# Routing layer 0's experts from each tile's best 32 tokens, with gate rows spread by DMA and the full comparison kept as a branch

## The chip, the cores and the metric

The kernel runs on one core of one Trainium2 chip. The metric is the device time of one execution in microseconds (us); the kernel before has a median of 1907.97 us over 3 runs. Engines are called PE (TensorE), DVE (VectorE), ACT (ScalarE), POOL (GpSimd) and SP (SyncE, which mostly issues DMAs). Most data is float32.

## The reference, cut to what matters

A sequence of 2048 tokens of 256 numbers passes through four layers. Each has a cross-attention over a context of 1601 rows and a feed-forward part, both added to x. What changes is the feed-forward part of layer 0, a set of 8 experts:

```python
t = log(clip(layernorm(x) @ gate_w, 1e-6))          # 2048 x 8
for _ in range(8):                                   # Sinkhorn
    t = t - logsumexp(t, over tokens); t = t - logsumexp(t, over experts)
gates = exp(t)
vals, idx = top_k(gates.T, 256)                      # each expert takes its best 256 tokens
out[e] = (layernorm(x)[idx[e]] @ experts[e]) * vals[e]
routed = zeros_like(x).at[idx].set(out)              # a token taken twice keeps one of its results
x = x + routed
```

The masks of layer 1 and layer 3 (2048 x 1601, the same for every token here) hide only some of the last 400 context rows.

## The kernel before

Tokens are held as 16 tiles of 128 partitions, four tiles to a chunk of 512. x stays on the chip from start to end. `network` calls the stages in order: `attention0`, then `experts0`, `attention1_tail`, `ffn1`, `attention1` of layer 2, `ffn2` with `attention3_keys`, `attention3_tail` and `ffn3`. While `attention0` runs, a helper looks at the masks (`look_at_masks`). `verdict` (L301) sums what it found into an integer, all engines read it, and a branch (`tc.If(n_odd == 0)`) stands between `attention0` and everything else: in the ordinary case attention 1 and 3 use only the last 400 context rows for the masked part, in the other branch all stages treat the masks in full. `experts0` is the first stage inside either branch.

`experts0` (L522 to L782) has its order on each engine written by hand (`manual_schedule`), with one generator, `ahead`, that holds the dense work: for each of the 16 tiles, four product steps of four matmuls (L589), which together give all 8 experts' outputs of the tile's 128 tokens. ACT copies each step out of PSUM (L599), and after every second step SP writes half a tile's table, 512 KB, to DRAM (L602). `step(ahead, 1)` places one product step at that point of the order; there are 64. The stages around it:

- The norm of four chunks (`norm_steps`: statistics L151, L152, `rstd` on POOL L157, `xn` L171, transposes L185) and gate logits (L626), with 6 product steps.
- Eight Sinkhorn iterations on the gates `g`, 128 x 16 x 8 (L639 to L652), with a step each.
- The ranking (L658 to L745): a token's rank for an expert is the number of tokens with a larger gate. For each expert the 2048 gates are spread to all partitions (16 PE transposes L670, 4 ACT copies L674 into `bc`). Then each tile's gates are compared with the row, as per-partition scalars. For nine tiles a comparison and a sum are one DVE instruction (L710); for seven tiles DVE compares (L715) and ACT sums (L689). Each pair of tiles is compared once: sums along the row give one side, and counting matmuls with `pick` (L682), four concurrent column groups, give the other. 50 product steps stand between.
- `rank` (L742 to L745), the winners (L751 to L767): who is under 256, and for each token the expert whose result counts, as an `index` into its tile's table and a `gate`.
- Sixteen indirect fetches on POOL (L772) and DVE's `add_row` (L782), x += row * gate.

The layer 1 stage `attention1_tail` begins with constants of the masks on DVE (L963 to L970), projections of 400 context rows (keys L983 and casts L988, values L992 and copies L996), then chunk by chunk norm and query matmuls (L1006). Weight scratch comes from pools whose buffers are freed in turn; in layer 3, `bv`, `bo`, `spread`, `wvT` belong to pools of attention 3, and the first loads of `ffn3` (L1965) follow when such room is free.

Of the kernel before, what the change touches and what calls it, by code (L numbers as in the profile page):

```python
# [54 lines left out]
class Net:  # L55
# [245 lines left out]
    def verdict(self):  # L301

        nc = self.nc
        n = self.const.tile([1, 1], mybir.dt.int32, name="n_odd")
        with ExitStack() as s:
            self.banks(s)
            ps = self.pm()
            nc.tensor.matmul(ps[0:1, 0:1], lhsT=self.some, rhs=self.ones[:, 0:1], start=True, stop=True)
            nc.vector.tensor_copy(n, ps[0:1, 0:1])
        return nc.values_load(n[0:1, 0:1], min_val=0, max_val=P)  # L310

# [210 lines left out]
    def experts0(self):  # L522
# [3 lines left out]
        for kc in range(2):  # L526
            (w,) = self.weights(f"e0{kc}", 2048)
            ew.append(w.rearrange("p (e f) -> p e f", e=E))
            nc.sync.dma_start(
                ew[kc], a["L0_ffn_experts"][:, kc * P : (kc + 1) * P, :].rearrange("e p f -> p e f")  # L530
            )

        short = 7
        with ExitStack() as s:
            self.banks(s)
            pool = s.enter_context(tc.tile_pool(name="e0", bufs=1))
            bcp = s.enter_context(tc.tile_pool(name="e0b", bufs=2))
            cp = s.enter_context(tc.tile_pool(name="e0c", bufs=9))  # L540
            stage = s.enter_context(tc.tile_pool(name="e0s", bufs=3))
            rows = s.enter_context(tc.tile_pool(name="e0r", bufs=6))
            dram = s.enter_context(tc.tile_pool(name="e0d", bufs=1, space=bass.MemoryType.DRAM))
            gw = pool.tile([P, 2, E], F32, name="gw")
            nc.sync.dma_start(gw, a["L0_ffn_gate_w"].rearrange("(k p) e -> p k e", p=P))

            after = pool.tile([P, (NT - short) * P], BF16, name="after")
            nc.gpsimd.memset(after, 1.0)
            nc.gpsimd.affine_select(
                out=after[:, :P], in_=after[:, :P], compare_op=ALU.is_gt, fill=0.0, base=0,  # L550
                pattern=[[1, P]], channel_multiplier=-1,
            )

            rest = pool.tile([P, NT], F32, name="rest")
            nc.vector.tensor_reduce(rest[:, 0:1], after[:, :P], AX.X, ALU.add)
            for t in range(NT - 1, -1, -1):
                nc.vector.tensor_scalar(rest[:, t : t + 1], rest[:, 0:1], float((NT - 1 - t) * P), None, ALU.add)

            first = pool.tile([P, 1], F32, name="first")
            nc.vector.tensor_scalar(first, rest[:, NT - 1 :], float(-E), float(E * (P - 1) - 1), ALU.mult, ALU.add)  # L560

            pick = pool.tile([P, E, E], BF16, name="pick")
            nc.vector.memset(pick, 0.0)
            for e in range(E):
                nc.vector.memset(pick[:, e, e : e + 1], 1.0)

            fold = pool.tile([P, E], F32, name="fold")
            nc.vector.tensor_reduce(
                fold, self.ident.rearrange("p (k r) -> p r k", k=4)[:, :E, :], AX.X, ALU.add
            )  # L570
            none = pool.tile([P, CH], BF16, name="none")
            nc.gpsimd.memset(none, 0.0)
            number = pool.tile([P, E], F32, name="number")
            for e in range(E):
                nc.vector.memset(number[:, e : e + 1], e + 1.0)
            xnT = [pool.tile([P, 2, CH], F32, name=f"xe{c}") for c in range(NCH)]
            table = [dram.tile([P * E, D], F32, name=f"table{t}") for t in range(NT)]
            g = pool.tile([P, NT, E], F32, name="g")

            near = pool.tile([P, NT, E], F32, name="near")  # L580
            far = pool.tile([P, short, E], F32, name="far")
            seen = pool.tile([P, NTOK], BF16, name="seen")
# [10 lines left out]

            def ahead():
                todo = None

                def out():
                    t, h, y, ps = todo
                    nc.scalar.copy(y[:, h * 512 : (h + 1) * 512], ps)  # L599
                    if h % 2:  # L600
                        at = slice((h - 1) * 512, (h + 1) * 512)
                        nc.sync.dma_start(table[t].rearrange("(p e) d -> p (e d)", e=E)[:, at], y[:, at])  # L602

# [35 lines left out]
            for _ in range(8):  # L639
# [12 lines left out]
                nc.vector.tensor_tensor(g, g, ri.unsqueeze(2).to_broadcast([P, NT, E]), ALU.mult)  # L652

# [44 lines left out]
            for e in range(E):  # L698
# [6 lines left out]
                for n, t in enumerate(turns):  # L705
# [21 lines left out]
                    if n in (1, 3, 7, 9, 11, 15) or n == 13 and e < 2:  # L727
                        step(ahead, 1)
# [3 lines left out]
            drain(ahead)  # L732
# [8 lines left out]
            for t in range(NT):  # L741
# [5 lines left out]

            taken = pool.tile([P, NT, E], F32, name="taken")
            order = pool.tile([P, NT, E], F32, name="order")
            top = self.small.tile([P, NT], F32, name="top")  # L750
            nc.vector.tensor_scalar(taken, rank, float(M), None, ALU.is_lt)  # L751
            nc.vector.scalar_tensor_tensor(
                order, rank, float(E), number.unsqueeze(1).to_broadcast([P, NT, E]), ALU.mult, ALU.add
            )
            nc.vector.tensor_tensor(order, order, taken, ALU.mult)
            nc.vector.tensor_reduce(top, order, AX.X, ALU.max)
            nc.vector.tensor_tensor(order, order, top.unsqueeze(2).to_broadcast([P, NT, E]), ALU.is_equal)
            nc.vector.tensor_tensor(order, order, taken, ALU.mult)
            nc.vector.tensor_tensor(g, g, order, ALU.mult)

            nc.vector.tensor_tensor(taken, order, number.unsqueeze(1).to_broadcast([P, NT, E]), ALU.mult)
            nc.vector.tensor_reduce(top, taken, AX.X, ALU.max)
            nc.vector.tensor_scalar(top, top, 1.0, first, ALU.max, ALU.add)
            index = pool.tile([P, NT], mybir.dt.uint32, name="index")
            nc.vector.tensor_copy(index, top)
            gate = pool.tile([P, NT], F32, name="gate")
            nc.vector.tensor_reduce(gate, g, AX.X, ALU.add)  # L767

            fetched = []
            for t in range(NT):  # L770
                row = rows.tile([P, D], F32, name="row")
                nc.gpsimd.indirect_dma_start(  # L772
                    row[:], None, table[t][:, :], bass.IndirectOffsetOnAxis(ap=index[:, t : t + 1], axis=0)
                )
                fetched.append(row)
                if t >= 2:
                    self.add_row(t - 2, fetched[t - 2], gate)
# [7 lines left out]
    def attention1(self, pre, mask=None, bias=False, beside=None):  # L785

        tc, nc, a = self.tc, self.nc, self.a
        raw = {}
        for n, w in zip(("Wk", "Wv", "Wq"), self.weights(pre, 512, 512, 512)):
            raw[n] = w.rearrange("p (o i) -> p o i", o=2)  # L790
            self.load_rows(f"{pre}_{n}", D, raw[n])
        with ExitStack() as s:
# [6 lines left out]
            for n in ("Wk", "Wv", "Wq"):  # L799
                wT[n] = kv.tile([P, 2, D], F32, name=f"{n}T")  # L800
# [146 lines left out]
    def attention1_tail(self, pre, mask, beside=None):  # L947

        tc, nc, a = self.tc, self.nc, self.a
        raw = {}  # L950
# [1123 lines left out]
```

## Time and profile before

| | us |
|---|---|
| median of 3 runs (lowest, highest) | 1907.97 (1907.56, 1908.0) |
| the profiled execution's own time | 1902.67 |
| its span, first to last instruction | 1900.9 |
| PE, DVE, ACT, POOL busy | 1744.6, 994.3, 819.8, 689.8 |
| mean granted clock of PE | 0.963 |
| gates before Sinkhorn ready | 746.4 |
| Sinkhorn | 746.6 to 765.6 |
| ranking, first row transpose to last counts | 766.6 to 905.25 |
| index of winners ready | 914.6 |
| last `add_row` ends | 937.5 |
| first query matmul of layer 1 | 943.98 |

All times within a profile are of the one profiled execution and run from its span's start. In a group's line come line, engine, operation, output and inputs, shapes and count, then busy time and mean duration, then the idle time of the engine ahead of these instructions with what ended it. In a line of windows the columns are the stretch, its length, the busy time of PE, PE's weight loads, DVE, ACT and POOL, the granted clock of PE as a share of full speed, the DMA engines' busy share, and GB/s.

### The profile page before, as it was taken

The page shows a single profiled execution, that of the slowest core. Times are in us where ns is not written, and L with a number is a line of the kernel's source. Part 1 is how long each engine was busy: PE and PEld are TensorE (multiplying, and loading weights), DVE is VectorE, ACT ScalarE, POOL GpSimd, SP SyncE. Part 2 cuts the span into 40 slices and gives each one's busy share as a digit, 9 for nine tenths or more (in the row PEclk, how much of TensorE's full clock was granted, in tenths as well). Part 3 has the DMA queues.
Part 4 walks back from the last instruction along what each step waited for, and adds up shares of the span by engine and source line. Part 5 has one row for each costly group of instructions (what it writes and reads, how often), then busy time and mean ns, then how long its engine had stood idle before and what let it go on. Part 6 is the DMA issues. An engine that isn't in the chain of part 4 may idle for free.

```text
span 1900.9 us, 22408 instructions
## 1 busy us (share of the span) xinstructions
PE 1744.6 (92%) x8397; PEld 868.1 (46%) x8397; DVE 994.3 (52%) x2022; ACT 819.8 (43%) x1097; POOL 689.8 (36%) x473
## 2 busy tenths in 40 slices
PE   6779999999999978999699989999999879999798
PEld 3223333333333335443345864645666722333587
DVE  5555654664465424899574653332115477886200
ACT  4554444443443432799123541121125546666222
POOL 2057876976786861000400561011015600211100
PEclk9889999999999998999699999999999989999799
DMA  8840000000000011222310000000000000000651
GB/s 274 271 143 1 1 1 1 1 1 1 1 1 1 1 58 65 89 100 100 118 39 0 1 26 0 1 0 1 0 6 1 6 16 19 20 21 13 198 184 44
DMA packets 51171, 86.70 MB, mean 46 GB/s; under 512 B 9949, under 2 KB 36974, under 8 KB 51054
## 3 DMA queue, kind: packets, MB, share of 16 engines
q1 hardware_dynamic: 48480, 81.45, 13.1%
q0 software_dynamic: 768, 2.10, 0.4%
q10 hardware_dynamic: 1806, 1.64, 0.3%
q8 instruction: 68, 1.11, 0.3%
q14 instruction: 49, 0.40, 0.1%
HBM read 61.96 MB, written 18.87 MB: 43 GB/s over the span
## 4 chain that ended last, share of the span: by engine, by line
PE 39%; DVE 4%; ACT 3%; issue 2%; POOL 2%; DMA 1%; SPq 1%; ACTq 0%; DVEq 0%; POOLq 0%
PE psc L913 5%; PE pa L933 5%; PE psc L1826 4%; PE psc L1978 3%; PE pa L1989 3%; ACT p L1833 2%; PE pa L1297 2%; PE pa L1050 2%; PE psc L1040 2%; PE pa L1843 2%; PE psc L1378 1%; PE pm L880 1%; PE pm L185 1%; PE psc L922 1%; PE psc L1244 1%
## 5 line engine op out<-in xcount | busy, mean ns | idle before, releaser
L492 POOL TENSOR_TENSOR sp<-sp,p 128x1024 f32<-128x1024 f32 (+1 forms) x176 | 418.4, 2377 | 56.2 <-ACT p L476 45.5
L396 DVE TENSOR_REDUCE mp<-pm 128x1 f32<-128x512 f32 x384 | 242.7, 679 | 175.1 <-PE pm L391 174.3
L476 ACT ACTIVATE p<-psc 128x1024 f32<-128x1024 f32 (+1 forms) x208 | 212.7, 1023 | 264.6 <-PE psc L471 176.0
L471 PE MATMUL psc<-qT,kT 64*128 64x512 f32 (+1 forms) x832 | 219.9, 592 | 0.0
L483 PE MATMUL pa<-p,v 128*64 128x512 f32 (+1 forms) x832 | 202.8, 609 | 0.0
L1833 ACT ACTIVATE p<-psc 100x1024 f32<-100x1024 f32 x128 | 124.3, 1020 | 61.3 <-PE psc L1826 54.0
L1811 DVE TENSOR_REDUCE ms<-psc 128x2 bf16<-128x800 f32 x128 | 124.1, 987 | 42.8 <-PE psc L1807 41.2
L589 PE MATMUL pa<-w_e,xe 128*128 128x512 f32 x256 | 124.8, 615 | 4.9 <-ACT y L599 4.9
L391 PE MATMUL pm<-kb,qb 64*128 64x512 bf16 x384 | 99.3, 392 | 25.9 <-DVE mp L396 22.2
L483 PEld LDWEIGHTS pa<-p,v 128*64 128x64 f32 (+1 forms) x832 | 50.9, 137 | 131.9 <-issue 128.9
L913 PE MATMUL psc<-q,kT 128*128 128x512 f32 (+1 forms) x208 | 102.2, 610 | 0.0
L933 PE MATMUL pa<-v,p 128*128 128x257 f32 (+1 forms) x416 | 95.3, 382 | 0.0
L471 PEld LDWEIGHTS psc<-qT,kT 64*128 64x128 f32 (+1 forms) x832 | 85.0, 185 | 20.1 <-issue 6.6
L1826 PE MATMUL psc<-q,kT 32*100 32x512 f32 x512 | 81.0, 645 | 13.4 <-ACT p L1833 11.7
L156 POOL TENSOR_SCALAR rstd<-mv 128x4 f32<-128x4 f32 x32 | 9.4, 297 | 227.9 <-DVE mv L152 215.8
L171 DVE TENSOR_SCALAR xn<-x,mv,rstd 128x256 f32<-128x256 f32 x128 | 59.0, 517 | 62.2 <-PE pm L185 47.9
L469 PE MATMUL psc<-sh,negz 64*128 64x512 bf16 (+1 forms) x416 | 86.7, 384 | 5.1 <-ACT sh L418 4.2
L885 DVE TENSOR_REDUCE mp<-pm 128x1 f32<-128x512 f32 x64 | 34.3, 570 | 102.5 <-PE pm L880 102.3
L689 ACT ACTIVATE seen<-ge 128x1152 bf16<-128x1152 bf16 (+6 forms) x56 | 83.8, 1496 | 0.3
L710 DVE SCALAR_TENSOR_TENSOR ge<-bc,g,after 128x128 bf16<-128x128 f32 (+8 forms) x128 | 77.9, 645 | 10.6 <-PE psc L682 8.3
L933 PEld LDWEIGHTS pa<-v,p 128*128 128x128 f32 (+1 forms) x416 | 77.5, 190 | 11.8 <-issue 0.2
L433 DVE RECIPROCAL ri<-ri 128x128 f32<-128x128 f32 x64 | 56.0, 920 | 46.0 <-ACT ri L429 46.0
(358 smaller groups left out, 2911.3 us busy)
## 6 DMA issues: line engine op xcount, KB each, us to landing
table<-y SPq DMA_DIRECT2D x32, 512.0 KB, 2.6
w<-in_L_ffn_w_dram SPq DMA_DIRECT2D x16, 1024.0 KB, 7.4
head<-in_mask_BxSxS_ik_dram SPq DMA_DIRECT2D x16, 600.5 KB, 4.3
head<-in_mask_1x1xSxS_ik_dram SPq DMA_DIRECT2D x16, 600.5 KB, 3.9
tail<-in_mask_BxSxS_ik_dram SPq DMA_DIRECT2D x16, 200.0 KB, 4.1
tail<-in_mask_1x1xSxS_ik_dram SPq DMA_DIRECT2D x16, 200.0 KB, 3.7
x<-in_x_dram SPq DMA_DIRECT2D x16, 128.0 KB, 3.6
w_e<-in_L_ffn_experts_dram SPq DMA_DIRECT2D x2, 1024.0 KB, 7.9
```

Of the source, the lines that this page charges most:

```text
L391: nc.tensor.matmul(pair[j][:, :wd], lhsT=qb[h, i * P : (i + 1) * P], rhs=kb[h, hp, k0 : k0 + wd], start=True, stop=True,)
L396: nc.vector.tensor_reduce(mp[:, i, j, n : n + 1], pair[j][:, :wd], AX.X, ALU.max)
L471: nc.tensor.matmul(sc[:r, j, :], lhsT=kT[h, hp, kt * P : kt * P + r], rhs=q[h, :], start=False, stop=True,)
L476: nc.scalar.activation(p[:r], sc[:r], AF.Exp, scale=DH**-0.5)
L483: nc.tensor.matmul(acc[h, :], lhsT=v[:r, kt, hp * P + h.start : hp * P + h.stop], rhs=p[:r, j, :], start=kt == 0, stop=kt == NKT - 1,)
L492: nc.gpsimd.tensor_tensor(sums[:r], sums[:r], p[:r], ALU.add)
L589: nc.tensor.matmul(ps, lhsT=xnT[t // TPC][:, kc, (t % TPC) * P : (t % TPC + 1) * P], rhs=ew[kc][:, 2 * h : 2 * h + 2, :], start=kc == 0, s ...
L913: nc.tensor.matmul(sc[:r, j, :], lhsT=kT[:, kc, ks], rhs=q[:, kc, :], start=kc == 0, stop=False)
L933: nc.tensor.matmul(acc[:, : D + 1], lhsT=p[:r, kt, i * P : (i + 1) * P], rhs=v[:r, kt, :], start=kt == 0, stop=kt == NKT - 1,)
L1811: nc.vector.tensor_reduce(ms[u % 2][:, i, 64 * k + DH : 64 * k + 64 : 32], ps[:, :, :NTAIL], AX.X, ALU.max)
L1826: nc.tensor.matmul(sc[j // 2][:TR, j % 2, :], lhsT=kT[h, g, kt * TR : (kt + 1) * TR], rhs=q[u][h, :], start=True, stop=True,)
L1833: nc.scalar.activation(p[:TR], sc[k][:TR], AF.Exp, scale=DH**-0.5)
```

## The change

The branch moves. `experts0` now runs directly behind `attention0`, ahead of the branch, and `verdict` is gone: what the look at the masks found becomes one of 18 numbers (`found`) that a matmul sums over partitions and DVE compares with constants (`right`). The others are, per expert, the number of winners (256) and the sum of their ranks (0 + ... + 255), and a count of equal neighbours among the best. Only if all 18 are as they should be does `n_odd` stay 0.

The ranking is replaced. All gates are transposed to 128 rows, one for each pair of a tile and an expert, and four `max` instructions (eight values each), with three `match_replace` between, give each row's best 32. Small matmuls turn these into `cand`: 512 candidates for each expert, 4 per partition. For each expert its row of 2048 gates is compared with four candidate columns (`is_lt`, four DVE instructions of 128 x 2048), and counting matmuls over all four give for every token the number of candidates above it. For a token whose larger rivals are all among the candidates, that count is its rank.

Gate rows of experts 1 to 7 no longer come through PE and ACT: the transposed gates are written to DRAM (`turned`) and read back to all partitions by one DMA for each expert. Expert 0's row is still transposed. The product steps stand elsewhere: 37 up to the matmul on `found`, and 27 inside the loop of fetches, each tile's fetch placed behind its own table.

If the test fails, `experts0_any` takes x and the gates from copies in DRAM (`kept`, sixteen DMAs of 128 KB; `gates`) and makes the former comparison with the same tables.

Layer 1's three weights are loaded ahead of the branch into `room`, a tile of 128 x 1536 for the whole program, which later holds layer 2's transposed weights, and layer 3's `wvT`, `bv`, `bo` and `spread`.

```diff
@@ experts0
-    def experts0(self):
+    def experts0(self, dram, ahead_of):
...
+        raw = self.raw_weights(*ahead_of)
...
+        BEST = 32
...
-            bcp = s.enter_context(tc.tile_pool(name="e0b", bufs=2))
-            cp = s.enter_context(tc.tile_pool(name="e0c", bufs=9))
+            bcp = s.enter_context(tc.tile_pool(name="e0b", bufs=3))
+            cp = s.enter_context(tc.tile_pool(name="e0c", bufs=8))
...
+            for t in range(NT):
+                nc.sync.dma_start(kept[t][:, :], self.x[t])
...
             zeros(True, False)
+            gT = pool.tile([P, P], F32, name="gT")
+            ps = self.pm()
+            nc.tensor.transpose(ps[:, :P], g.rearrange("p t e -> p (t e)"), self.ident)
+            nc.vector.tensor_copy(gT, ps[:, :P])
+            nc.sync.dma_start(turned.rearrange("t e n -> (t e) n"), gT)
+            nc.sync.dma_start(gates[:, :], g.rearrange("p t e -> p (t e)"))
+
+            def row(e):
+                bc = bcp.tile([P, NTOK], F32, name="bc")
+                if e:
+                    nc.sync.dma_start(
+                        bc.rearrange("p (t n) -> p t n", t=NT), turned[:, e, :].partition_broadcast(P)
+                    )
+                return bc
+
+            bcs = [row(0)]
...
+            bcs.extend((row(1), row(2)))
...
+            for k in range(BEST // 8):
+                top8 = best[:, 8 * k : 8 * k + 8]
+                nc.vector.max(top8, at)
+                if k < BEST // 8 - 1:
+                    nc.vector.match_replace(left[k % 2], top8, at, -1.0)
+                    at = left[k % 2]
...
+            step(ahead, 1)
+            for e in range(E):
+                bc, four = bcs.pop(0), []
+                for k in range(4):
+                    ge = cp.tile([P, NTOK], BF16, name="ge")
+                    nc.vector.tensor_scalar(ge, bc, cand[:, k, e : e + 1], None, ALU.is_lt)
+                    four.append(ge)
+                    if k == 0 and late is not None:
+                        count(*late)
+                    if k % 2:
+                        step(ahead, 1)
+                late = e, four
+                if e + 3 < E:
+                    bcs.append(row(e + 3))
...
+            count(*late)
+            zeros(False, True)
+            step(ahead, 1)
...
+            step(ahead, 5)
+            ps = self.pm()
+            nc.tensor.matmul(ps[0:1, : 2 * E + 2], lhsT=self.ones[:, 0:1], rhs=found, start=True, stop=True)
...
+            nc.vector.scalar_tensor_tensor(
+                right, ps[0:1, : 2 * E + 2], 1.0, right, ALU.mult, ALU.not_equal, accum_out=odd
+            )
+            nc.vector.tensor_copy(n_odd, odd)
+
+            fetched = []
+            for t in range(NT):
+                while made[0] <= t:
+                    step(ahead, 1)
+                self.fetch(rows, fetched, table, index, t)
+                if t >= 2:
+                    self.add_row(t - 2, fetched[t - 2], gate)
+            for t in range(NT - 2, NT):
+                self.add_row(t, fetched[t], gate)
+        return n_odd, (table, kept, gates), raw
@@ attention 3 (attention3_keys)
-        bv = self.broadcast(kv, a["L3_xattn_bv"], D, "bv3")
-        bo = self.broadcast(kv, a["L3_xattn_bo"], D, "bo3")
+        bv, bo = room[:, 512 : 512 + D], room[:, 768 : 768 + D]
+        nc.sync.dma_start(bv, a["L3_xattn_bv"].partition_broadcast(P))
+        nc.sync.dma_start(bo, a["L3_xattn_bo"].partition_broadcast(P))
...
-        wvT = kv.tile([P, 2, D], F32, name="wvT")
+        wvT = room[:, :512].rearrange("p (k i) -> p k i", k=2)
@@ network
-    n_odd = net.verdict()
+    room = ctx.enter_context(tc.tile_pool(name="w1", bufs=1)).tile([P, 1536], F32, name="w1")
+    dram = ctx.enter_context(tc.tile_pool(name="e0d", bufs=1, space=bass.MemoryType.DRAM))
+    odd, again, raw = net.experts0(dram, ("L1_xattn", room))
+    n_odd = tc.nc.values_load(odd[0:1, 0:1], min_val=0, max_val=P)
     with tc.If(n_odd == 0) as masked:
-        net.experts0()
...
-            net.attention1_tail("L1_xattn", masks[0], later)
+            net.attention1_tail("L1_xattn", masks[0], raw, later)
...
     with masked.Else():
-        net.experts0()
-        net.attention1("L1_xattn", mask=masks[0])
+        net.experts0_any(*again)
+        net.attention1("L1_xattn", mask=masks[0], room=room)
```

## The prediction, made before the result was known

> **What bounds the kernel now.** I read the page's first part, then busy time by stage around layer 0's experts, then the groups of that stretch with shapes apart, then timelines at its two ends, and last the waits of SP's queue.
>
> ```profile
> PE 1744.6 (92%) x8397; PEld 868.1 (46%) x8397; DVE 994.3 (52%) x2022; ACT 819.8 (43%) x1097; POOL 689.8 (36%) x473
> ```
>
> TensorE is busy for 92% of the span, so time goes only where PE loses work or idles. By stage (columns: window, length, then busy us of PE, weight loads, DVE, ACT, POOL, then granted clock, DMA share, GB/s):
>
> ```profile
> core 0: us, PE busy (x) PEld busy (x) DVE busy (x) ACT busy (x) POOL busy (x), PEclk, DMA share, GB/s
> 640.00:692.00 52.00, 50.26 (x254) 16.59 (x250) 18.92 (x29) 23.94 (x26) 46.63 (x21) 1.00 0.00 1
> 709.00:715.50 6.50, 0.00 (x0) 0.00 (x0) 4.32 (x46) 0.00 (x0) 1.27 (x2) 0.69 0.85 263
> 715.50:722.50 7.00, 5.71 (x24) 4.78 (x24) 5.32 (x20) 1.17 (x2) 1.26 (x2) 0.50 0.00 0
> 722.50:728.70 6.20, 6.20 (x9) 2.70 (x10) 1.20 (x6) 0.58 (x1) 1.26 (x2) 0.51 0.00 0
> 728.70:742.40 13.70, 13.02 (x65) 8.47 (x64) 5.03 (x18) 4.30 (x8) 1.26 (x2) 1.00 0.20 78
> 770.00:895.00 125.00, 120.13 (x585) 51.05 (x584) 116.72 (x289) 113.36 (x178) 0.00 (x0) 1.00 0.24 97
> 895.00:942.00 47.00, 28.76 (x119) 15.50 (x117) 26.78 (x73) 14.24 (x24) 18.11 (x21) 0.73 0.44 142
> ```
>
> In the ranking (770 to 895) PE, DVE and ACT are all near full: cutting one alone gives little. Before it PE stands still for 6.5 us and then runs at half clock to 728.7; behind it PE is busy 61%. The groups of 692 to 945 (shapes, count, then busy us and mean ns):
>
> ```profile
> L589 PE MATMUL pa<-w_e,xe 128*128 128x512 f32 x256 | 124.8, 615 | 4.9 <-ACT y L599 4.9
> L682 PE MATMUL psc<-ge,pick 128*8 128x512 bf16 x224 | 26.9, 379 | 0.0
> L670 PE MATMUL pm<-ident,g 128*128 128x128 f32 x128 | 20.0, 282 | 0.2 <-ACT bc L674 0.2
> L715 DVE TENSOR_SCALAR ge<-bc,g 128x1920 bf16<-128x1920 f32 x8 | 9.7, 1213 | 0.0
> ```
>
> The products (L589) are work of PE that stays. PE timeline at the two ends (start, us, then the idle time ahead), and SP's queue ahead of the last FFN:
>
> ```profile
> 715.76 0.71 PE L185 MATMUL pm<-ident,xn 128*128 128x128 f32 x2 [6.77 <-DVE xn L171]
> ...
> 941.76 2.19 PE L185 MATMUL pm<-ident,xn 128*128 128x128 f32 x8 [8.08 <-DVE xn L171]
> 943.98 2.93 PE L1006 MATMUL pm<-xnT,WqT 128*128 128x512 f32 x3
> ```
> ```profile
> SPq L1965 <- POOL x L1888: 8.2, 1, 8.2
> ```
>
> **The change part by part**, in the times of the profiled execution: it took 1902.67 us, 5.3 below the median of the runs shown (1907.97).
>
> *(a) Branch moved behind the experts.* Attention 0's last matmuls end at 709.0, and until 715.76 PE waits for the constants of the ranking and the first chunk's statistics on DVE. Without a branch between, these are issued among attention 0's last DVE work, and the two expert loads ahead of it on SP. PE then goes on at 709.05 and stays warm. A chunk of four tiles takes 6.86 us when warm (728.70 to 735.57), while 715.76 to 728.70 took 12.94 for the same. So the gates, ready at 746.4, come 6.7 + 6.1 = 12.8 earlier. The cover for the hoisted DVE work is attention 0's PE work (50.3 of 52 us busy, DVE 18.9); were it gone, up to 6.8 comes back. The branch itself cost under 1 us (the integer cast ended at 702.5, the first w_e issue came at 703.35) and costs that again later.
> SP gets sixteen copies of x to DRAM (128 KB each, at 0.3 to 0.6 us of issue): 5 to 10 us of its queue, behind gw and ahead of the first table write; that write is some 15 us later, so nothing waits.
> Rule against row: "TensorE: Matmul & The Clock Gate", section "What's actually happening", in the Trainium skill has the clock come back after one busy window of about 3.4 us. The rows show 0.50 and 0.51 through 13 us after the gap. By the rule the lost half clock is some 1.7 us and (a) gives 8.4; by the rows it gives 12.8. I take the rows, here and for the gap in (d).
>
> *(b) Sinkhorn* is unchanged: 746.6 to 765.6 becomes 733.8 to 752.7.
>
> *(c) The comparison.* Removed: 128 + 56 DVE comparisons (77.9 us of L710 and about 67 of L715), 56 ACT sums (83.8 + 11.3), 112 of 128 transposes of gate rows on PE (17.5 of 20.0) and 28 of their 32 ACT copies. Added: one PE transpose, a copy, two small DMAs, then four searches for eight maxima and three replacements on 128x128. The trace has no such operation; the nearest rows are 128x128 operations at 0.28 to 0.35. I take 0.3 each (2.1 together), with bounds of 1.5 and 4.2. First comparison at 757.5.
> The loop: 32 comparisons of 2048. L715 grows by 0.52 ns an element (1213 at 1920, 1147 at 1792), so 1.28 alone; these starts overlap the end of the one before, and start to start at 1920 was 1.13, so 1.20 here: 32 x 1.20 = 38.4 (bound above 41). PE does per expert two product steps (four L589 each; eight took 3.6 to 3.7) and 16 counts in four column groups (about 1.03): 4.6 against DVE's 4.8. DVE bounds it, closely.
> Gate rows of experts 1 to 7 come by DMA: each 1 MB in 2048 runs of 512 B, on SP's queue with the table writes (0.52 MB per expert). The first is issued after the turned gates have landed, at about 757 plus 2, and is needed at 762.3. A 1 MB load took 5.7 (w_fc, 1024 runs of 1 KB), so it is 2 to 3 late. Later rows are asked for three experts ahead. Rate: two expert loads together, 2048 runs of 1 KB, landed in 7.9. If a run costs the same whatever its size, a row needs about 5.5 of transfer, with the table's 1.3 (0.52 MB at 400 GB/s) 6.8 per expert, 2 over the loop's 4.8: 14 in seven rows. If a run costs by its bytes, 2.8 + 1.3 is hidden. Here a rule speaks: "DMA: Bandwidth & Descriptors", "Why small descriptors are slow (HBM only)", gives a packet about 3 cycles beside its 32-byte beats: 19 cycles for 512 B against 35 for 1 KB, so 3.0 + 1.3 = 4.3, hidden. No row here has 512 B runs. Its "Specifications" put the HBM limit of a core near 358 GB/s, and the loop asks 1.57 MB in 4.8 = 327: nearly all. I charge 3 for the first row and later jitter (bounds 0 and 14); a late row stops DVE, then counts, while PE goes on with at most the steps already in order.
> Then zeros, two copies of the counts (1.2), the fold (32 matmuls, 4.4), twelve small DVE operations and three more (15 x 0.3): index at about 810. Five steps cover the chain on PE (8.6), the test's matmul follows, and its verdict is ready at 816. The 27 steps left take 27 x 1.72 = 46.5: products end at 862, 865 with the 3. Check by PE work from 752.7: 50 steps x 1.72 = 86.0, counts 8.2, fold 4.4, zeros 1.7, transposes and small ones 3.1: 103.4, and 109 with the idle starts. The same stretch took 905.25 - 766.3 = 138.9. Gain 30, less 3.
>
> *(d) The tail.* Before: from 905.25 to the first query matmul of layer 1 (943.98) 38.7 us, with sixteen fetches at 1.25 in it that nothing covered. Now fetches run under the remaining products; behind the last product remain its copy (0.6), table write (2.6), fetch (1.0 + 2.8) and add (0.5): 7.5. Then the branch (1), and behind it what could be early before: three key constants (2.2 on DVE), statistics and xn of chunk 0 (DVE 2.3, POOL 1.4, DVE 1.4), key casts, four value copies, and the 2.26 reduction of w_fc, which is now loaded behind the branch (5.7, beside these). PE has 12 + 8 + 16 matmuls (3.5 + 3.7 + 6.9) that pass through two buffers emptied by this DVE queue, partly at half clock. I make it 19.5 behind the add: 27 in all (bounds 20 and 36). Gain 11.7.
>
> *(e) Elsewhere.* Layer 3's bv, bo and wvT now lie in a tile kept for the whole program. In the trace SP stands 8.2 before the first load of the last FFN, since that room was freed by attention 3's output; PE is busy 25.0 of 35 us in 1755 to 1790. Loads now go out before that, and 16 of its matmuls stand among attention 3's last ones. Gain 8 (bounds 0 and 13). bv and bo wait for layer 2's attention, where SP stood anyhow (254.9 us on L933): nothing, or their 5 us if that cover were gone.
>
> Sum: 12.8 + 30 - 3 + 11.7 + 8 = 59.5. 1902.67 - 59.5 = 1843.2; with the 5.3, 1848.5.
>
> **The rivals.**
> 1. Transfers set the loop: 6.8 per expert and later table writes, 14 instead of 3, with part of it again where fetches wait for tables. For: 327 GB/s asked. Against: 350 to 430 GB/s seen. Gain 38 to 48: about 1865.
> 2. What moved behind the branch eats the tail: (d) gives nothing and (a) only the rule's 8.4, (e) little. Gain 27 to 40: about 1874. For: DVE's long order there, and clock 0.73.
> 3. Slower: the other branch runs. It is taken if one of the 18 sums differs from its constant: a tie, more than 32 of one tile's 128 tokens in an expert's best 256, or masks unlike the ones before. Price: the old comparison again with no products beside it. DVE alone was busy 116.7 there, so some 115 + 25 against the 59.5, at least 80 slower (1990), and attention over all keys on top. Against: the mean is 16 of 128, and 32 lies over four deviations (3.7) away; the trace of before shows its masks take the short branch. In the same place, if a row took over 13 us (4.8 + 60/7), the loop would eat the whole gain.
> 4. It doesn't do what it says: product steps do not fill the wait for rows, and PE idles as it does now. That is rival 1 or 2 in size.
>
> **How the numbers follow.** Forecast 0.64 (own range 1833 to 1862), rival 1 0.17, rival 2 0.11, slower 0.05 (0.03 the branch, 0.02 the rows), near nothing 0.03. Within 0.2% (3.8 us) is about what a measurement of this kernel can't tell from no change. Faster 0.93, same 0.02, slower 0.05. The range 1829 to 1877 takes in rivals 1 and 2.
>
> **What would show it.** Right: L185 straight behind attention 0 at clock 1.00; TENSOR_SCALAR 128x2048 x32 near 1.28 with under 4 us idle for rows; fetches under L589; L1965 with no 8 us wait. Wrong: DVE waiting over 10 us for DMA rows, PE idle in the loop, over 36 us from the last product to the first query matmul, or a second comparison behind the branch.

## The result, and the profile after

| | before | after |
|---|---|---|
| median (us), 6 runs each | 1908.95 | 1896.9 |
| lowest, highest | 1907.56, 1915.22 | 1890.57, 1902.9 |
| span of the profiled execution | 1900.9 | 1897.0 |

The ratio is 0.993, 95% interval 0.9905 to 0.9955: 0.7% faster, where 3.1% had been forecast. The medians are 12.1 us apart, but the two profiled executions only 3.9. The account below is made between these two, so its sum has to come to 3.9.

By stage, where the stages are cut at the start of Sinkhorn (first `cs`), at its end, at the end of the last product, and at layer 1's first query matmul:

| stretch | before | after | change | predicted |
|---|---|---|---|---|
| start to Sinkhorn | 746.6 | 737.0 | -9.6 | -12.8 |
| Sinkhorn | 19.0 | 19.8 | +0.8 | 0 |
| ranking and products | 139.6 | 161.1 | +21.5 | -27 |
| tail to the first query matmul | 38.7 | 30.7 | -8.1 | -11.7 |
| the rest | 956.9 | 948.5 | -8.4 | -8 |

Attention 0's last projections start within 0.4 us of each other in these two executions (703.1 and 702.8); in the other executions of the same code they start anywhere from 702.1 to 708.3, so one execution alone doesn't fix the first row. Four of the five are within 4 us of their forecast. The ranking is 48 us off. The page's first part, and busy time by stage (columns as before):

```profile
PE 1729.4 (91%) x8090; PEld 858.4 (45%) x8102; DVE 916.8 (48%) x1743; ACT 725.8 (38%) x957; POOL 690.2 (36%) x477
```
```profile
709.00:713.50 4.50, 3.95 (x24) 3.62 (x25) 3.50 (x13) 1.07 (x2) 0.00 (x0) 0.79 0.09 29
713.50:719.50 6.00, 6.00 (x10) 2.55 (x11) 0.19 (x1) 0.59 (x1) 1.28 (x2) 0.59 0.00 0
719.50:726.30 6.80, 6.46 (x33) 4.22 (x32) 3.46 (x13) 2.15 (x4) 1.27 (x2) 1.00 0.21 80
757.00:775.00 18.00, 13.46 (x65) 6.23 (x64) 7.60 (x16) 5.76 (x10) 0.00 (x0) 1.00 0.30 76
775.00:850.00 75.00, 48.10 (x159) 15.82 (x159) 34.23 (x30) 7.03 (x12) 0.00 (x0) 0.78 0.66 145
871.00:918.00 47.00, 47.00 (x114) 20.96 (x114) 6.69 (x17) 15.93 (x28) 8.82 (x10) 1.00 0.51 185
918.00:949.00 31.00, 15.01 (x44) 8.77 (x43) 15.22 (x47) 4.49 (x11) 5.04 (x8) 0.72 0.40 127
```

In the comparison (775 to 850) no engine is full: PE is busy 64%, DVE 46%, the clock is at 0.78, and the DMA engines move 145 GB/s, under half of the 327 that the prediction asked of them. The groups of 690 to 960, and the row of the DMA issues (name, issues, size, median us to landing):

```profile
L559 PE MATMUL pa<-w_e,xe 128*128 128x512 f32 x256 | 129.8, 661 | 0.0
L702 DVE TENSOR_SCALAR ge<-bc,cand 128x2048 bf16<-128x2048 f32 x32 | 39.0, 1282 | 48.6 <-DMA bc<-turned 42.1 <-PE pa L559 6.4
L692 PE MATMUL psc<-ge,pick 128*8 128x512 bf16 x128 | 21.9, 513 | 30.7 <-DVE ge L702 30.7
```
```profile
bc<-turned SPq DMA_DIRECT2D x7, 1024.0 KB, 17.5
```

The comparisons take what was forecast (1282 ns each), but DVE stands 48.6 us ahead of them, 42.1 of it put down to gate rows, which land 17.5 us after their issue. PE stands 30.7 for DVE in turn, with only two product steps per expert in its order. The DVE timeline gives the beat, one row every 11 to 12 us:

```profile
761.60 4.87 DVE L702 TENSOR_SCALAR ge<-bc,cand 128x2048 bf16<-128x2048 f32 x4
775.43 4.88 DVE L702 TENSOR_SCALAR ge<-bc,cand 128x2048 bf16<-128x2048 f32 x4 [8.96 <-DMA bc<-turned]
787.07 4.87 DVE L702 TENSOR_SCALAR ge<-bc,cand 128x2048 bf16<-128x2048 f32 x4 [6.76 <-DMA bc<-turned]
798.22 4.87 DVE L702 TENSOR_SCALAR ge<-bc,cand 128x2048 bf16<-128x2048 f32 x4 [6.28 <-DMA bc<-turned]
```

The tail, from PE's timeline, then SP's, then the chain that ended last:

```profile
917.71 0.60 PE L225 MATMUL pm<-ident,w 128*128 128x128 f32 x4
...
939.05 2.03 PE L1162 MATMUL pm<-WvT,ctxT 128*100 128x256 f32 x4 [10.58 <-DVE kb L1158]
942.11 5.29 PE L1162 MATMUL pm<-WvT,ctxT 128*100 128x256 f32 x12 [1.04 <-DVE kb L1158]
947.24 1.34 PE L185 MATMUL pm<-ident,xn 128*128 128x128 f32 x8
948.52 3.70 PE L1176 MATMUL pm<-xnT,WqT 128*128 128x512 f32 x8
```
```profile
919.04 0.38 SPq L214 DMA_DIRECT2D w_fc<-in_L_ffn_w_fc_dram  x1
919.51 0.88 SPq L214 DMA_DIRECT2D w_pr<-in_L_ffn_w_proj_dram  x1
```
```profile
922.38 7.29 DMA row<-table,index
929.69 0.49 DVE x L947
```

SP is past the branch before the last fetch, and issues 2 MB of weights at 919. The fetch of 922.4 then takes 7.3 us from issue to landing; the last one of before took 2.8:

```profile
934.20 2.78 DMA row<-table,index
```

Behind the branch PE waits 10.6 us for a key cast that stands on DVE behind the last add, the constants, the statistics and `xn`.

### The profile page after: what moved, and what is told of

The parts are those of the page before. It is cut to its first block, busy times and chain, and to the rows that moved or that the text cites. A ratio compares the mean times of both kernels' runs of the same rounds, so it can differ in the third digit from the quotient of the medians.

```text
span 1897.0 us, 21306 instructions
## 1 busy us (share of the span) xinstructions
PE 1729.4 (91%) x8090; PEld 858.4 (45%) x8102; DVE 916.8 (48%) x1743; ACT 725.8 (38%) x957; POOL 690.2 (36%) x477
## 4 chain that ended last, share of the span: by engine, by line
PE 68%; DVE 12%; DMA 8%; ACT 5%; issue 3%; POOL 3%; SPq 0%; ACTq 0%; DVEq 0%; POOLq 0%
PE pa L472 8%; PE psc L460 6%; PE psc L1078 5%; PE pa L1098 5%; PE pa L559 5%; PE psc L1998 4%; DVE mp L385 3%; DMA bc<-turned 3%; PE psc L2150 3%; PE pa L2161 3%; DVE ri L422 3%; PE psc L458 2%; PE pm L380 2%; PE pa L1467 2%; ACT p L2005 2%
## 5 line engine op out<-in xcount | busy, mean ns | idle before, releaser
L559 PE MATMUL pa<-w_e,xe 128*128 128x512 f32 x256 | 129.8, 661 | 0.0
L1998 PE MATMUL psc<-q,kT 32*100 32x512 f32 x512 | 83.1, 659 | 13.2 <-ACT p L2005 11.5
L460 PEld LDWEIGHTS psc<-qT,kT 64*128 64x128 f32 (+1 forms) x832 | 85.3, 185 | 19.8 <-issue 6.6
L572 ACT COPY y<-pa 128x512 f32<-128x512 f32 x64 | 37.6, 587 | 145.5 <-PE pa L559 141.8
L808 POOL DMA_INDIRECT row<-table,index x16 | 15.4, 965 | 182.6 <-DVE rank L730 138.5
L559 PEld LDWEIGHTS pa<-w_e,xe 128*128 128x128 f32 x256 | 52.7, 214 | 64.3 <-issue 63.6
## 6 DMA issues: line engine op xcount, KB each, us to landing
bc<-turned SPq DMA_DIRECT2D x7, 1024.0 KB, 17.5
```

The source lines that it names most:

```text
L460: nc.tensor.matmul(sc[:r, j, :], lhsT=kT[h, hp, kt * P : kt * P + r], rhs=q[h, :], start=False, stop=True,)
L559: nc.tensor.matmul(ps, lhsT=xnT[t // TPC][:, kc, (t % TPC) * P : (t % TPC + 1) * P], rhs=ew[kc][:, 2 * h : 2 * h + 2, :], start=kc == 0, s ...
L1998: nc.tensor.matmul(sc[j // 2][:TR, j % 2, :], lhsT=kT[h, g, kt * TR : (kt + 1) * TR], rhs=q[u][h, :], start=True, stop=True,)
```

## The experiments

All kernels below are the changed kernel with one edit, except where said; the cuts show its main lines, and `...` stands for lines left out. Results with an interval are medians of four executions or more, and their ratio is to the kernel before; those without are single executions. A "run" of 512 B is one contiguous piece that one partition reads; "shared" means that all 128 partitions read the same pieces, "own" that each reads its own.

**Is the row the whole loss? (norow)**

```diff
-            bcs.extend((row(1), row(2)))
...
-                bc, four = bcs.pop(0), []
+                bc, four = bcs[0], []
...
-                if e + 3 < E:
-                    bcs.append(row(e + 3))
...
```

> Left out: the gate rows of experts 1 to 7; all eight experts are compared with expert 0's row, so there is no row transfer at all, and the short branch is taken whatever the test finds. This is the loop as the prediction costed it, without the row: if the rows are the whole loss, the 32 comparisons take 38 to 41 us from first to last, PE has no idle time over 1 us in the loop, the products end 43 to 49 us earlier than at 917.7, and the run is near 1850. If something else holds the loop as well (counts, product steps, the cold clock), it stays over 55 us.

Measured: 1845.7 us. The loop is the forecast one, without a gap, and the last product ends 107.5 us behind Sinkhorn (109 had been forecast without the charge of 3 for rows; the changed kernel took 161.1):

```profile
760.54 38.36 DVE L701 TENSOR_SCALAR ge<-bc,cand 128x2048 bf16<-128x2048 f32 x32
```

So counts, steps and clock hold nothing up by themselves: the transfers are the loss, 53.6 us in this stage.

**What about a row is slow? Runs and sharing (rows8k, own512, own8k)**

```diff
-        turned = dram.tile([NT, E, P], F32, name="turned")
+        turned = dram.tile([E, NT, P], F32, name="turned")
...
-                        bc.rearrange("p (t n) -> p t n", t=NT), turned[:, e, :].partition_broadcast(P)
+                    nc.sync.dma_start(bc, turned[e].rearrange("t n -> (t n)").partition_broadcast(P))
```

> The changed kernel, with the turned gates laid out in DRAM by expert, so that each gate row is read as one run of 8 KB per partition (128 runs of 8 KB instead of 2048 of 512 B); the same row is still read 128 times. In the changed kernel a row landed 17.5 us after its issue, two in flight, and the period per expert was 11.5 us, of which DVE compared for 4.9. Theory A (the many small runs cost): rows land in 4 to 7 us, DVE's waits for rows fall from 42 us to under 8, the products end some 40 us earlier, and the time falls to about 1855. Theory B (the same DRAM bytes read by all 128 partitions cost): period stays at 11 to 12 us, time near 1897. Theory C (the shared queue with the table writes holds the rows up): period stays near 11.

Measured: 1848.8 us (1841.2 to 1856.1), ratio 0.9664 (0.9631 to 0.9697). Rows land in 8.0 us at the median and DVE never waits for one:

```profile
767.40 38.36 DVE L700 TENSOR_SCALAR ge<-bc,cand 128x2048 bf16<-128x2048 f32 x32
```

Next, rows of the experts' weights in place of the gates:

```diff
...
+                    own = a["L0_ffn_experts"].rearrange("e (q r) f -> (e q) r f", q=16)
+                    nc.sync.dma_start(bc.rearrange("p (t n) -> p t n", t=NT), own[:, :, :P])
```

> Left out: experts 1 to 7 get no gate rows; in their place each partition reads 16 runs of 512 B of its own (1 KB apart) out of the experts' weights, the same number of runs and bytes from different addresses, and the short branch is taken whatever the test finds. Theory A (small runs): nothing changes, period 11 to 12 us and some 42 us of DVE waiting. Theory B (same bytes read by all): waits under 8 us in all, period 5 to 6. Theory C (queue shared with table writes): nothing changes.

The same with one run of 8 KB per partition:

> Left out: experts 1 to 7 get no gate rows; each partition reads one run of 8 KB of its own out of the experts' weights, and the short branch is taken whatever the test finds. Theories A (small runs) and B (same bytes read by all): no waits to speak of, period about 4.9 to 5.5 us. Theory C (shared queue, bytes alone): period stays near 11 us.

Measured: 1853.6 and 1848.0 us; 1.1 us and nothing of waiting for rows. The small runs alone are not slow (theory A falls), the shared source alone is not (B falls), and the queue with the table writes is not (C falls). It takes two things together. own512, DMA issues:

```profile
bc<-in_L_ffn_experts_dram SPq DMA_DIRECT2D x7, 1024.0 KB, 8.6
```

**More places for the source (copies8, copies16)**

```diff
+                    for c in range(8):
+                        nc.sync.dma_start(
+                            bc[16 * c : 16 * (c + 1)].rearrange("p (t n) -> p t n", t=NT),
+                            turned[c][:, e, :].partition_broadcast(16),
+                        )
```

> Runs of 512 B as in the changed kernel, but the turned gates are written to eight places in DRAM, and each place is read by 16 partitions only (eight DMAs of 16 partitions for each row instead of one of 128). Neither small runs of other data nor one row of 8 KB runs read by all was slow, so what is left is the two together. Theory D (512 B at one place of DRAM read 128 times in a row is served slowly): with 16 readers at a place the rows land in 6 to 10 us, DVE waits under 10 us for them in all, and the run is near 1855. Theory E (what costs is how one DMA of 128 x 16 runs with a repeated source is spread over the engines): each of the smaller DMAs is just as slow, period still 11 us, time near 1895.

Measured: 1885.1 us; DVE waits 23.9 us for rows and 7.3 for table writes, a row every 9 us. Between the two theories, and nearer to E: of the changed kernel's 48.6 us of waiting 33.3 stay, about two thirds.

```diff
+                    for q in range(8):
+                        nc.sync.dma_start(
+                            bc[16 * q : 16 * (q + 1)].rearrange("p (t n) -> p t n", t=NT), turned[:, :, e, :]
+                        )
```

> The turned gates lie 16 times in DRAM (one DMA of 1 MB writes them), and each row comes by eight DMAs of 16 partitions, as in the run with eight places; but here the 16 partitions of one DMA read 16 different places, where there all 16 read the same. Same runs of 512 B, same number of DMAs. Theory F (runs that the engines read at the same place at the same time wait for each other): rows no longer late, period 4.9 to 6 us behind the first row, near 1858 (the first row comes 3 to 5 us later, behind the 1 MB write). Theory E (small DMAs or small runs from this kind of source): period stays near the 9 us of the run with eight places, near 1885.

Measured: 1885.0 us, 19.9 us of waits for rows and 6.5 for tables, 30.1 in all: hardly better than with eight places. Theory F falls as it was put: that the partitions of a transfer read different copies at one time hardly helps. But both kernels leave the runs of a copy 4 KB apart, and in the second the copies lie 64 KB apart, a multiple of that. This led to the next experiments.

**Distance of the runs in DRAM (rows2k, own4k, gap1k, gap2k, pad4k5)**

```diff
+        turned = dram.tile([NCH, E, TPC, P], F32, name="turned")
...
+                        turned[:, e].rearrange("c i n -> c (i n)").partition_broadcast(P),
```

> The turned gates laid out so that a row is four runs of 2 KB per partition (512 runs), read by all 128 partitions from the same place. Theory D (the time is that of repeated reads at one small place): between the two, rows in 8 to 13 us, DVE waiting 0 to 20 us in all. A cost per run alone would have it at a quarter of the excess of the changed kernel, some 10 us of waits.

Measured: 1860.1 us, waits of 8.7 us, of which 5.0 for the first row. This layout changed two things: the runs are 2 KB long, and they lie 16 KB apart.

```diff
+                    own = a["L3_ffn_w1"].rearrange("e (q r) f -> (e q) r f", q=16)
+                    nc.sync.dma_start(bc.rearrange("p (t n) -> p t n", t=NT), own[:, :, :P])
```

> Left out: experts 1 to 7 get no gate rows; each partition reads 16 runs of 512 B of its own out of the last FFN's weights, whose rows are 4 KB long, so the runs lie 4 KB apart as in the turned gates (where the run of own data before had them 1 KB apart); the short branch is taken whatever the test finds. Theory G (512 B out of every 4 KB: the distance of the runs in DRAM is what is slow): period 9 to 12 us, 30 us or more of DVE waiting, near 1890. Theory H (small runs of a source that all partitions share): period 4.9 to 6 us, under 8 us of waiting, near 1853.

Measured: 1845.5 us, 0.5 us of waits. The distance alone is not slow.

```diff
+        turned = dram.tile([E, NT, 2, P], F32, name="turned")
...
+                        bc.rearrange("p (t n) -> p t n", t=NT), turned[e, :, 0, :].partition_broadcast(P)
```

> The real gate rows in runs of 512 B, all partitions reading the same 16 runs, but the turned gates lie by expert with 512 B left empty behind each run, so that the runs are 1 KB apart instead of 4 KB. Theory G (distance of the runs): rows in time, period 4.9 to 6 us, near 1853. Theory H (shared source and small runs): as the changed kernel, period 11 us, 40 us of waits, near 1897.

Measured: 1853.0 us, 3.9 us of waits. So H falls as well as G: the same 2048 runs of 512 B, read by all partitions, are in time when they lie 1 KB apart. What was slow is small shared runs at 4 KB distance.

```diff
-        turned = dram.tile([NT, E, P], F32, name="turned")
+        turned = dram.tile([NT, E + 1, P], F32, name="turned")
...
-            nc.sync.dma_start(turned.rearrange("t e n -> (t e) n"), gT)
+            nc.sync.dma_start(turned[:, :E, :], gT)
```

> The changed kernel with one row of 512 B left empty in the turned gates for each tile, so that a gate row's 16 runs lie 4.5 KB apart instead of 4 KB; all else is the same (real gate rows, 2048 runs of 512 B, read by all partitions). If it is that the 16 shared runs all lie at multiples of 4 KB from each other, rows land in time: period 4.9 to 6 us, under 10 us of waits, about 1852. If shared runs far from each other are slow whatever the exact distance, nothing changes: period 11 us, 1897.

The other layout, with the runs 2 KB apart, is `[E, NT, 4, P]`, filled and read at index 0 of the third axis.

> The turned gates by expert with the 16 runs of a row 2 KB apart. By multiples: 2 KB puts the runs at two places within 4 KB instead of one, and a row should cost between the one with 1 KB (in time) and the changed kernel (11 us): period 5 to 8 us, 5 to 25 us of waits, 1853 to 1875. If only distances of 4 KB and more are slow, it is in time.

Measured: 1848.7 us (1841.7 to 1853.9) with the pad, ratio 0.9677 (0.9644 to 0.9711), and 1866.0 at 2 KB. The rows of the comparisons by form (pad4k5), and the first gaps at 2 KB and with the pad on DVE's timeline:

```profile
L702 DVE TENSOR_SCALAR ge<-bc,cand 128x2048 bf16<-128x2048 f32 x32 | 38.7, 1281 | 2.2 <-DMA bc<-turned 2.1
```
```profile
769.23 4.87 DVE L702 TENSOR_SCALAR ge<-bc,cand 128x2048 bf16<-128x2048 f32 x4 [3.89 <-DMA bc<-turned]
776.42 4.88 DVE L702 TENSOR_SCALAR ge<-bc,cand 128x2048 bf16<-128x2048 f32 x4 [2.32 <-DMA bc<-turned]
```
```profile
770.76 9.66 DVE L702 TENSOR_SCALAR ge<-bc,cand 128x2048 bf16<-128x2048 f32 x8 [1.32 <-DMA bc<-turned]
780.79 19.25 DVE L702 TENSOR_SCALAR ge<-bc,cand 128x2048 bf16<-128x2048 f32 x16 [0.37 <-DMA bc<-turned]
```

One empty row of 512 B per tile takes DVE's wait for rows from 42.1 us to 2.1, with the same number and size of transfers. The runs lie further apart and are fast, so distance as such is not what costs. That the shared runs fall on few places within 4 KB (one at 4 KB distance, two at 2 KB, four at 1 KB, eight with the pad) fits the rows with 512 B below; larger multiples of 4 KB were not measured with runs of 512 B, and in rows2k, with runs of 2 KB at 16 KB, most of the loss is gone:

| source of a row | run | distance | median landing | DVE waits for rows |
|---|---|---|---|---|
| shared (the change) | 512 B | 4 KB | 17.5 | 42.1 |
| shared, gap2k | 512 B | 2 KB | 13.5 | 17.0 |
| shared, gap1k | 512 B | 1 KB | 9.1 | 3.9 |
| shared, pad4k5 | 512 B | 4.5 KB | 8.7 | 2.1 |
| shared, rows2k | 2 KB | 16 KB | 9.9 | 8.7 |
| shared, rows8k | 8 KB | one run | 8.0 | 0 |
| own data, own512 | 512 B | 1 KB | 8.6 | 1.1 |
| own data, own4k | 512 B | 4 KB | 8.6 | 0.5 |

**Rows without DMA (transposed)**

```diff
+                    if nxt is not None:
+                        row(e + 1, nxt, k)          # 4 transposes on PE, one copy on ACT
```

> The changed kernel with all gate rows made as in the kernel before, by 16 PE transposes and 4 ACT copies for each expert, placed in the loop one chunk ahead of each comparison; no row DMA. PE pays 7 x 2.5 us and DVE no longer waits: if the row transfer is the loss, PE bounds the loop at 7 us per expert (two steps 3.44, counts 1.03, transposes 2.5), products end near 881, and the time is about 1865, 15 above the version with 8 KB runs. If it stays above 1885, something besides the transfers holds the loop.

Measured: 1857.1 us (1850.6 to 1858.8), ratio 0.9705 (0.9671 to 0.9739), 8 us under the expectation. An expert takes 6.3 us instead of 7 (so PE's transposes cost less than the 2.5 charged), and PE is full (window, columns as above):

```profile
757.00:812.00 55.00, 54.17 (x335) 28.52 (x336) 42.22 (x46) 27.49 (x51) 0.00 (x0) 1.00 0.22 88
```

Rows on PE cost some 8 us more than rows by DMA that are in time, and some 40 less than rows by DMA at 4 KB distance.

**Parts of the change alone, on the kernel before (branch_only, room_only)**

```diff
-    n_odd = net.verdict()
+    odd = net.verdict()
+    net.experts0()
+    n_odd = tc.nc.values_load(odd[0:1, 0:1], min_val=0, max_val=P)
```

> The kernel before with one part of the change: the verdict is still formed behind attention 0, but the experts run ahead of the branch, with the old comparison. By the prediction's (a) the gates are ready 12.8 us earlier; the changed kernel showed 8.9. Behind the branch the first constants and layer 1's weights come later. The gates should come 9 to 13 us earlier and the run should be 3 to 10 us faster; if the tail takes it all back, no difference.

Measured: 1917.6 us, ratio 1.004 (1.0025 to 1.0055): slower, against the expectation. Sinkhorn starts at 738.8, 7.9 us earlier and under the 9 to 13 expected (the changed kernel's gain, by the cuts of the table above, is 9.6), but behind the branch (waits, longest last):

```profile
PE pm L225 <- DMA w_L_xattn<-in_L_xattn_Wk_dram: 31.6, 1, 31.6
```

Layer 1's weights are then issued behind the last fetches and PE stands 31.6 us; the first query matmul comes at 960.5 instead of 944.0. What the branch's move brings in front is lost behind it unless those weights are loaded ahead of the branch, as the change does.

The other part alone: the change's `room` in layers 2 and 3, with `verdict`, branch and `experts0` of before.

> The kernel before with one part of the change: the tile for the whole program that holds layer 2's transposed weights and layer 3's wvT, bv, bo and spread; branch, experts and layer 1's weights as before. By the prediction's (e) the last FFN's first load no longer waits 8.2 us for attention 3's output: 8 us faster (1900 against 1908), bounds 0 and 13. If the 8.4 us that the changed kernel gained behind layer 1's first query matmul came from elsewhere, there is no difference here.

Measured: 1900.9 us (1900.0 to 1902.3), ratio 0.9943 (0.9926 to 0.9959): some 11 us, within the bounds of 0 to 13. SP's first load of the last FFN goes out at 1760.9 (before: 1774.7), and its longest wait is 3.3 (on PE), where one of 8.2 stood for attention 3's output. First before, then this kernel:

```profile
1774.65 0.39 SPq L1965 DMA_DIRECT2D w<-in_L_ffn_w_dram  x1
...
1760.85 0.41 SPq L1973 DMA_DIRECT2D w<-in_L_ffn_w_dram  x1
```

**The tail, and a version that beats both (rows8k_act, rows8k_both)**

```diff
-                nc.vector.tensor_copy(kb[:, o, :], ps[:, :NTAIL])
+                nc.scalar.copy(kb[:, o, :], ps[:, :NTAIL])
...
-                nc.vector.tensor_copy(v[:TR, kt, 0:D], ps[:TR, :D])
+                nc.scalar.copy(v[:TR, kt, 0:D], ps[:TR, :D])
```

> The version with 8 KB runs, and the copies of layer 1's keys (kb) and values out of PSUM on ACT instead of DVE. In the changed kernel PE stood 10.6 us for a kb cast that lay on DVE behind the last add, the constants, the statistics and xn of chunk 0 and the reduction of w_fc. If that order is what makes the tail, the time from the last product to the first query matmul falls from 30 us to 20 to 23, and the run from 1849 to about 1840. If the statistics' chain on DVE sets it alone, nothing moves.

Measured: 1842.2 us, ratio 0.9641 (0.9624 to 0.9659), and from the last product to the first query matmul 21.5 us where rows8k had 29.8.

```diff
-        self.load_rows("L1_ffn_w_fc", D, wfc)
-        self.load_rows("L1_ffn_w_proj", F, wpr)
...
         yield
+        self.load_rows("L1_ffn_w_fc", D, wfc)
+        self.load_rows("L1_ffn_w_proj", F, wpr)
+        yield
```

> The same, and the loads of layer 1's FFN weights (2 MB) one step later. In the changed kernel SP issued them at 919.0 and 919.5 and the last fetch, issued at 922.4, took 7.3 us against 3.3 before. If the fetch waited for the DMA engines behind those loads, it takes 3 to 4 us again and the last add comes 3 to 4 us earlier: 1836 or so. If w_fc is then late for its reduction, part of it comes back.

Measured: 1840.1 us (1830.8 to 1843.6), ratio 0.9608 (0.9577 to 0.9639). PE's timelines, first of rows8k_act and then of rows8k_both:

```profile
863.52 0.60 PE L225 MATMUL pm<-ident,w 128*128 128x128 f32 x4
...
883.17 2.20 PE L185 MATMUL pm<-ident,xn 128*128 128x128 f32 x8 [4.99 <-DVE xn L171]
885.20 4.26 PE L1174 MATMUL pm<-xnT,WqT 128*128 128x512 f32 x8
```
```profile
869.33 0.60 PE L225 MATMUL pm<-ident,w 128*128 128x128 f32 x4
...
883.87 1.64 PE L185 MATMUL pm<-ident,xn 128*128 128x128 f32 x8 [0.35 <-DVE xn L171]
885.75 3.70 PE L1174 MATMUL pm<-xnT,WqT 128*128 128x512 f32 x8 [0.24 <-ACT xnT L189]
```

With the loads later the last add starts 6.9 us behind the last product (12.0 without), and the tail is 16.3 us. The last fetch takes 2.8 again, as in the kernel before (2.8 by its line above, not 3.3):

```profile
873.50 2.81 DMA row<-table,index
```

So both waits named in the profile after, for the key casts and for the fetch, were real. The intervals of these two kernels overlap, so of the second edit's worth in the whole run only the tail's 5 us is shown.

## Why the prediction was wrong

- **The step that failed** is the term for the gate rows in (c): 3 us, bounds 0 and 14. DVE stood 48.6 us, 42.1 of it named as rows, and against norow the stage is 53.6 us longer. The upper bound was made from loads in which every run has an address of its own (5.5 us for two expert loads, 43 ns for each of 128 runs of 1 KB on 16 engines), and taken as the worst case for a run. Here a row came every 11.5 us (six from 775.4 to 844.2); less 1.3 for its table write that is 10.2 us, by the same estimate 80 ns for a run of half the size. The text noted that no row of the trace had 512 B runs; that no row had many reads of a few places was not noted, nor did I look at where these places lay.
- **The rule on small descriptors.** The estimate from it (the Trainium skill, "DMA: Bandwidth & Descriptors", "Why small descriptors are slow (HBM only)") had the rows hidden, at 4.3 us per expert. With the pad the same 2048 runs of 512 B are hidden, but for 2.1 us in all. So its verdict held for the size of the run, though no experiment isolates its 3.0 us for a row; that section prices size, not places.
- **The rivals.** Rival 1 named the right resource, with a price of 14 that was a third of the loss. What rival 4 says came with it: PE was busy only 64% in the loop. The point from which rows eat the whole gain, 13 us each, was about right: at 11.5 us a row, 3.9 us are left between the profiled executions and 12.1 between the medians, which puts that point at 12 to 13. Rival 2 did not come (the tail gained 8.1), nor did the other branch run; the low end of rival 2, a gain of 27, is 1881 and lay outside the range said to take it in.
- **The rest of (c) was right.** Maxima cost 0.29 each, the comparisons 38.4 us for 32 (norow), verdict to last product 46.6. (The 67 us of L715 in the list of what is removed are 57, by its forms in the trace; they enter no sum.)
- **A match that is partly luck.** With the pad or with 8 KB runs the kernel takes 1848.7 and 1848.8, where 1848.5 was forecast. Between the profiled executions of before and pad4k5 the first stage gains 6.9 for a forecast of 12.8 and the tail 8.6 for 11.7, while the ranking gains 29.7 for 27 and the rest 11.3 for 8; misses in both directions cancel.
- **(a) gave 9.6, not 12.8.** PE goes on at 709.17 as forecast, but not warm: the clock is 0.79 and then 0.59 to 719.5, and the first chunk takes 10.3 us instead of 6.9. In own4k, whose code up to here is the same, the clock stays at 1.00 from 704 on and the chunk takes 7.0 (PE, first of the changed kernel, then of own4k):

```profile
709.17 1.09 PE L185 MATMUL pm<-ident,xn 128*128 128x128 f32 x8 [0.52 <-DVE x L436]
...
713.54 6.11 PE L559 MATMUL pa<-w_e,xe 128*128 128x512 f32 x8
719.48 1.04 PE L185 MATMUL pm<-ident,xn 128*128 128x128 f32 x8
```
```profile
710.66 1.09 PE L185 MATMUL pm<-ident,xn 128*128 128x128 f32 x8 [0.52 <-DVE x L436]
...
714.11 3.68 PE L559 MATMUL pa<-w_e,xe 128*128 128x512 f32 x8
717.63 1.04 PE L185 MATMUL pm<-ident,xn 128*128 128x128 f32 x8
```

From the last projections to Sinkhorn own4k and gap2k take 30.8 us, 12.7 less than before (43.5) and so all of the forecast; the other executions of this code take 32.4 to 35.9. What sets the clock in one execution stays open. The 8.4 estimated from the rule of the Trainium skill ("TensorE: Matmul & The Clock Gate", "What's actually happening") was nearer to 9.6 in number only: it priced the cold stretch of before, and the miss lies in a cold stretch of the changed kernel.

- **(d) gave 8.1, not 11.7.** I had said that w_fc's load runs beside the rest; it collided with the last fetch, which took 7.3 us. The prediction had 3.8, with 1.0 for the issue added to a 2.8 that already held it.
- **(e) was right**, and its size is known to a few us: 8.4 in the profile of the change and 11 between the medians of room_only, for a forecast of 8. The stretch behind the first query matmul took 948.5 here, 945.6 in pad4k5 and 953.6 in transposed, with the same code.

## What to carry to other kernels

The price of a transfer that spreads one row to all partitions depended here on where its runs lay, not only on their size and bytes: keep a shared source contiguous (8.0 us to landing), or pad it so that small runs do not lie 4 KB apart (8.7 with the pad, 17.5 without). When an operation has no near row in the trace, ask what is new in it besides its size, and let the bound cover that. Work moved ahead of a branch needs the loads of what follows moved with it, and a queue that passes the branch early starts loads that the last transfers ahead of it then meet.

## What was not expected of the hardware

Sixteen runs of 512 B, each read by 128 partitions, took about 11 us per 1 MB row when they lay 4 KB apart (17.5 us from issue to landing, up to two rows in flight). At 4.5 KB, and in one run of 8 KB, they were in time behind comparisons of 4.9 us; 2 KB lay between (a row every 7 to 8 us). Own data at 4 KB distance (2048 places instead of 16) was not slow. That few places of the memory serve all reads at such distances would fit, but what in the memory does this no experiment shows. With eight or sixteen copies 33.3 and 30.1 of the 48.6 us of DVE's waiting stayed; those kernels also changed the number of transfers, so how much the places did is open. More product steps inside the loop, to cover late rows, were not tried.
